# An order of its own for a conv and attention kernel: every engine's line from the kernel's list scheduler

## The chip, the cores and the metric

The kernel runs on one core of one Trainium2 chip. The metric is device time of one launch in microseconds (us). One core has five engines that each work through a line of instructions of their own: TensorE (PE in the profile, its weight loads PEld), VectorE (DVE), ScalarE (ACT), GpSimd (POOL) and SyncE (SP), which here only issues DMAs. Semaphores tie the lines together.

## The reference

The input is 8 images of 384 channels, 32 x 32 (1024 tokens). All is float32. Two layers follow each other:

```
layer 0:  xn = rmsnorm(x);  u, z = xn @ Win            (forward and flipped)
          u = silu(causal_conv4(u));  dt, Bm, Cm = u @ Wx
          delta = softplus(dt @ Wdt + b);  dA = exp(delta * A)
          h[t] = dA * h[t-1] + delta * u * Bm[t]       (16 states per channel)
          y = (sum_n h * Cm + u * D) * silu(z) @ Wout
          x = x + 0.5 * (0.25 * (y_fwd + y_bwd) + sigmoid(dwconv3x3(xn)) * xn)
layer 1:  t = t + attention(layernorm(t))              (6 heads of 64, causal)
          t = t + ffn(layernorm(t))                    (384 -> 1536 -> 384)
```

The FFN's weights are replaced by their signs, and its activations are scaled by a maximum per image group of one; it applies to the first five images only (`FFN_B`), the others get zero. The recurrence over 1024 tokens, two directions, 384 channels and 16 states is the bulk of the elementwise work.

## The kernel before

Channels lie on the 128 partitions in three chunks (c), tokens in two halves of 512 (h). For each image there are three stages.

`before_scan` (L323) does the norm, the in-projection (`in_proj`, L352), the causal conv in both directions d (`conv`, L366; on DVE for image 0, as products with diagonal matrices for the others), Silus, the projection to dt, Bm and Cm (`project`, L500) and `delta` (L530). Its results go to DRAM: u, the Bm and Cm rows (L525), delta and delta*u (L553). `gates` (L460) does the depthwise conv (`local`, L399), z's Silu and the residual.

The scan works in units. One unit covers one image b, one part (direction and half), one chunk c, one group j of four states and one pair q of channel blocks: 128 partitions are 32 channels x 4 states. There are 8 x 4 x 3 x 4 x 2 = 768 units. For each, SP loads delta and delta*u broadcast over states (`s_load`, L587) and the rows (`s_row`, L602); POOL multiplies by Bm (`s_first`, L617), ACT takes two exponentials into PSUM (L630), DVE runs two scans (L638), ACT keeps the carry (L643), POOL multiplies by Cm (L644), PE sums the states of two units by four products that stand on four column strips of the array (`s_sum`, L657), and DVE gates the result (L680, L687). There are six g buffers, so POOL can be ahead of PE by a few units only.

`attention` (L694) and `feed_forward` (L1006) follow an image's scan: out-projection (L723), layernorm, q and k (L756), v (L774), scores of two heads (L816, contraction 64, so each uses half of the array's rows), masked row maximum on DVE (L829), exponential on ACT (L849), transposes (L899), weighted values of two heads (L913), projection (L973); then the two FFN products (L1031, L1075) with their quantization in between and a Gelu (L1054).

What sets the order: every stage hands over a list of steps with rough lengths. The steps of images' other stages are spread between the scan units by due times (end of the kernel function), and each unit's operations get a priority 600 ahead (`ahead_of_all`, L1149). The framework then reorders all instructions by priority in a simulated timeline and assigns buffers in rotation. Here and there `pin` keeps a few instructions in program order, and `at_once` (L269) gives the second product of a pair a head start of 400, so that both come close together. PSUM has eight banks of 128 x 512: two for the scan's exponentials, one for y, and five for the rest by purpose:

```
102:    BANKS = {"y": 1, "da": 2, "s": 2, "pt": 2, "av": 1}
```

The program begins with image 0's `before_scan` alone (only its gates and z are put beside the scan), then runs image 0's scan beside image 1's to 3's `before_scan` and the binarizing of the FFN weights (`binarize`, L207), then the rest; the attention of the last image's second half is last (L1220).

## Time and profile before

| | us |
|---|---|
| median of 3 runs (4350.55 to 4361.42) | 4356.6 |
| the profiled execution | 4362.3 |
| its span, first to last instruction | 4360.0 |
| PE busy | 3692.8 |
| POOL busy | 3596.6 |
| DVE busy | 3378.7 |
| ACT busy | 2805.2 |
| mean granted PE clock (share of full) | 0.876 |

A row of a timeline has the start, the duration, engine, source line, operation, output <- input with shapes, the count merged in that row, and in brackets the idle time before it with what ended it. A row of the waits has who waited for whom, the total, how often and the longest. A row of stretches has from:to, its length, busy time with count for PE, PEld, DVE, ACT and POOL, then the clock, the DMA share and GB/s. A group has its total, and the mean of one in ns. Each float32 product of the PE appears as two matmul records, so an x count of 2 is one product.

### The profile page before, as it was taken

How to read it: one execution, taken by the hardware profiler on the slowest of the kernel's cores; microseconds unless marked ns; L12 is line 12 of the kernel's file. 1: busy time of each engine (PE TensorE's matmuls, PEld its weight loads, DVE VectorE, ACT ScalarE, POOL GpSimd, SP SyncE). 2: the span in 40 equal slices, each digit the busy share in tenths (PEclk: the TensorE clock that was granted, in tenths of full speed). 3: DMA queues.
4: the chain of work that ended last, by engine and by line, in shares of the span. 5: the costliest groups of instructions: out<-in, count | busy, mean ns of one | idle time of the engine just before them, and what ended most of it. 6: DMA issues, size and time to landing. Idle time of an engine off the chain costs nothing.

```text
span 4360.0 us, 43528 instructions
## 1 busy us (share of the span) xinstructions
PE 3692.8 (85%) x12522; PEld 1416.7 (32%) x12522; DVE 3378.7 (77%) x4712; ACT 2805.2 (64%) x5379; POOL 3596.6 (82%) x1560
## 2 busy tenths in 40 slices
PE   3487877898987998779998799898899996999899
PEld 1132322333332333223333233333334332343344
DVE  6899899777988679986789866898877676577723
ACT  4778687676776667765767656677575574575435
POOL 0688989998989988898988998898998989899900
PEclk7686968899987989888999798998889898899899
DMA  6646465422455324463243641346423224224200
GB/s 214 237 162 206 171 231 174 167 95 93 169 193 180 116 78 163 148 230 116 74 163 131 220 150 68 121 148 211 167 91 131 70 92 168 80 83 157 103 15 29
DMA packets 334151, 612.01 MB, mean 140 GB/s; under 512 B 34088, under 2 KB 92888, under 8 KB 333912
## 3 DMA queue, kind: packets, MB, share of 16 engines
q1 hardware_dynamic: 324256, 593.10, 40.0%
q10 hardware_dynamic: 9656, 16.15, 1.1%
q8 instruction: 98, 1.61, 0.2%
q14 instruction: 141, 1.16, 0.1%
HBM read 443.45 MB, written 165.68 MB: 140 GB/s over the span
## 4 chain that ended last, share of the span: by engine, by line
PE 48%; DVE 22%; ACT 6%; issue 5%; POOL 4%; DMA 3%; SPq 0%; DVEq 0%; ACTq 0%; POOLq 0%
DVE g L638 11%; PE s L816 8%; PE yp L1075 6%; PE pt L899 5%; PE qp L756 5%; PE av L913 5%; PE y L657 5%; PE hp L1031 3%; PE op L723 3%; POOL g L617 2%; DVE loc L416 2%; PE in L357 2%; PE ap L973 2%; DVE u L385 2%; POOL g L644 2%
## 5 line engine op out<-in xcount | busy, mean ns | idle before, releaser
L617 POOL TENSOR_TENSOR g<-ud,bc 128x1024 f32<-128x1024 f32 x768 | 1825.1, 2377 | 341.3 <-DMA ud<-sud 131.8
L644 POOL TENSOR_TENSOR g<-g,bc 128x1024 f32<-128x1024 f32 x768 | 1821.9, 2372 | 206.5 <-ACT carry L643 105.1
L630 ACT ACTIVATE da<-dl,amat 128x512 f32<-128x512 f32 x1536 | 1053.2, 690 | 739.7 <-DVE g L638 723.1
L638 DVE TENSOR_TENSOR_SCAN g<-da,carry,g 128x512 f32<-128x512 f32 x768 | 942.9, 1268 | 169.4 <-POOL g L617 120.5
L638 DVE TENSOR_TENSOR_SCAN g<-da,g 128x512 f32<-128x512 f32 x768 | 896.0, 1207 | 147.3 <-POOL g L617 114.5
L816 PE MATMUL s<-k,q 64*128 64x512 f32 (+3 forms) x1152 | 492.9, 608 | 72.0 <-DVE nm L829 70.5
L829 DVE CUSTOM_DVE_ANT_0 pr<-s,cmask 128x512 f32<-128x512 f32 (+3 forms) x576 | 306.1, 551 | 303.1 <-PE s L816 256.4
L657 PE MATMUL y<-g,gather 128*32 128x512 f32 x3072 | 469.3, 687 | 62.0 <-POOL g L644 56.7
L1075 PE MATMUL yp<-h,w 128*128 128x512 f32 x720 | 342.0, 630 | 53.9 <-DVE h L1057 39.9
L902 ACT COPY ptn<-pt 128x512 f32<-128x512 f32 (+3 forms) x576 | 261.6, 477 | 190.2 <-PE pt L899 188.1
L1031 PE MATMUL hp<-t,w 128*128 128x512 f32 x720 | 341.2, 622 | 44.6 <-DMA w<-w1s 22.2
L899 PE MATMUL pt<-ident,pr 128*128 128x128 f32 x1728 | 335.1, 309 | 18.4 <-ACT ptn L902 15.5
L357 PE MATMUL in<-xn,win 128*128 128x512 f32 x576 | 288.8, 647 | 54.1 <-DVE xn L348 18.1
L899 PEld LDWEIGHTS pt<-ident,pr 128*128 128x128 f32 x1728 | 204.5, 150 | 382.6 <-ACT ptn L902 131.6
L537 PE MATMUL dp<-xd,wdt 25*128 25x512 f32 x192 | 162.7, 968 | 154.2 <-ACT du L550 132.9
L416 DVE SCALAR_TENSOR_TENSOR loc<-xn,vec,loc 128x496 f32<-128x496 f32 (+3 forms) x384 | 265.5, 717 | 20.5 <-ACT loc L405 18.6
L849 ACT ACTIVATE pr<-pr,low 128x512 f32<-128x512 f32 (+3 forms) x384 | 241.5, 630 | 53.7 <-DVE low L843 53.1
L913 PE MATMUL av<-ptn,v 128*64 128x512 f32 (+3 forms) x1152 | 265.4, 531 | 1.7 <-ACT ptn L902 1.6
L756 PE MATMUL qp<-t,wqk 128*128 128x512 f32 x576 | 254.8, 597 | 6.8 <-DVE t L318 6.7
L816 PEld LDWEIGHTS s<-k,q 64*128 64x128 f32 x1152 | 165.1, 209 | 263.5 <-DVE nm L829 159.4
L1075 PEld LDWEIGHTS yp<-h,w 128*128 128x128 f32 x720 | 140.7, 201 | 257.7 <-issue 185.9
L1031 PEld LDWEIGHTS hp<-t,w 128*128 128x128 f32 x720 | 136.5, 197 | 246.5 <-issue 150.9
(152 smaller groups left out, 4360.9 us busy)
## 6 DMA issues: line engine op xcount, KB each, us to landing
dl<-sdl SPq DMA_DIRECT2D x384, 256.0 KB, 3.3
ud<-sud SPq DMA_DIRECT2D x384, 256.0 KB, 4.3
bc<-rows SPq DMA_DIRECT2D x256, 256.0 KB, 3.9
su<-u SPq DMA_DIRECT2D x48, 512.0 KB, 3.0
du<-su SPq DMA_DIRECT2D x96, 256.0 KB, 4.4
sdl<-du SPq DMA_DIRECT2D x96, 256.0 KB, 3.5
sud<-du SPq DMA_DIRECT2D x96, 256.0 KB, 3.4
t<-st SPq DMA_DIRECT2D x39, 512.0 KB, 5.2
```

The costliest lines, as they stand in the source:

```text
L357: nc.tensor.matmul(out=mp, lhsT=st["win", c][:, k, i, :], rhs=st["xn"][:, k, half(h)], start=(k == 0), stop=(k == NC - 1),)
L617: pin(nc.gpsimd.tensor_tensor(g, ud, rows_for(u, 0), ALU.mult))
L630: nc.scalar.activation(da, sst["dl", u.b, u.c, u.part, u.q][:, i, :], AF.Exp, scale=amat[:, u.c, k, u.j : u.j + 1],)
L638: nc.vector.tensor_tensor_scan(gi[:, ::step], da[:, ::step], gi[:, ::step], first, ALU.mult, ALU.add)
L644: pin(nc.gpsimd.tensor_tensor(g, g, rows_for(u, 1), ALU.mult))
L657: mm = nc.tensor.matmul(out=y[k * BLK : (k + 1) * BLK, :], lhsT=gather, rhs=pair[k // 2][:, k % 2, :], start=(u.j == u.first_group), stop= ...
L756: nc.tensor.matmul(out=qp, lhsT=st["wqk"][:, c, o : o + P], rhs=st["xn"][:, c, half(h)], start=(c == 0), stop=(c == NC - 1),)
L816: mm = nc.tensor.matmul(out=ss[e][:, : k1 - k0], lhsT=st["q"][rows_of(e), c, chunk(qi)], rhs=st["k"][rows_of(e), c, k0:k1], start=True, st ...
L899: nc.tensor.transpose(pt[:, chunk(i)], pr[:, e, chunk(j % QT)], ident)
L913: mm = nc.tensor.matmul(out=av[rows_of(e), cols], lhsT=st["v"][:, j, hd * HD : (hd + 1) * HD], rhs=st["ptn", j, e][:, cols], start=(j == 0 ...
L1031: nc.tensor.matmul(out=hp, lhsT=st["w1"][:, c, chunk(m % 2)], rhs=st["xn"][:, c, half(h)], start=(c == 0), stop=(c == NC - 1),)
L1075: nc.tensor.matmul(out=yp, lhsT=st["w2", k // 6][:, k % 6, :], rhs=st["h", k // NC][:, k % NC, half(h)], start=(k == 0), stop=(k == NF - 1),)
```

## The change

The kernel no longer calls the engines. Its operations go to a recorder (`Plan`), which notes for each the tiles it reads and writes, its place in the program as a rank (minus the head start that `hurry` gives), and a price in us. `place` then simulates the five engines: at each moment a free engine takes the ready operation of lowest rank whose buffers are to be had; `emit` issues the result in that order, with the framework's own reordering off. Operations recorded under `together` are one unit: the four y products, the two score products, the two weighted-value products, the two projections, each group of Silus or Gelus with the table load behind it. The order of the y products is now 0 to 3. Buffers are given out by the plan too: a free one of the kind, not the next in rotation, within a window of as many tiles as the pool has (PSUM may go beyond the window when one more is free).

The five banks "s", "pt" and "av" become one kind, "any". Operations named `nc.any` go to whichever of ACT and DVE takes them first.

Image 0 gets a `lead`: the norm, in-projection, conv, Silu, projection and delta of half 0, forward, stand alone at the beginning; all else of image 0 goes beside its scan. For this u and the rows are stored by halves (`keep_u`, `keep_rows`), and x is loaded by halves.

```diff
+class Op:
+    def __init__(self, name, what, args, kwargs, rank):
+        self.name, self.parts, self.rank = name, [(what, args, kwargs)], rank
+        self.before, self.behind, self.left = {}, [], 0
+        self.tiles = []
+        self.ready, self.start, self.end = 0.0, None, None
+        self.time = 0.0
+
...
+
...
+    def together(self):
+        self.group = []
+        yield
+        self.group = None
+
...
+    def record(self, name, what, args, kwargs):
...
+        if self.group:
+            op = self.group[0]
+            op.parts.append((what, args, kwargs))
+        else:
+            op = Op(name, what, args, kwargs, len(self.ops) - self.sooner)
+            self.ops.append(op)
+            if self.group is not None:
+                self.group.append(op)
...
+            op.time = max(op.time, cost)
+        else:
+            op.time += cost
+        for v in views:
+            t, box = v.tile, v.box()
...
+                t.order = len(t.kind.queue)
+                t.kind.queue.append(t)
+            for other, b in t.writes + (t.reads if write else []):
+                if other is not op and not (b[1] < box[0] or box[1] < b[0] or b[3] < box[2] or box[3] < b[2]):
+                    op.before[id(other)] = other
...
+    def cost(self, name, what, args, kwargs, written, views):
+
+        if what == "dma_start":
+            n = max(v.free() * v.shape[0] for v in views)
+            return n * 4 / 250e3
+        n = max([v.free() for v in views] or [0])
+        if what == "preload_act_table_set":
+            return 2.6
+        if name == "tensor":
+            return 2 * max(written[0].free(), 64) * 0.00084 / 0.9 + 0.01
+        if name == "gpsimd":
+            return 0.05 + n * 0.00221
+        if name == "scalar":
+            return 0.15 + n * 0.00087 + (0.1 if "accum_out" in kwargs else 0.0)
+        if what == "tensor_tensor_scan":
+            return 0.095 + n / 480
+        if what == "tensor_scalar" and n > HB:
+            return 0.09 + n * 0.00082
+        return (0.17 if "accum_out" in kwargs else 0.085) + n / 960
...
+    def place(self):
+        engines = self.ENGINES
+        waiting = {e: [] for e in engines}
+        ready = {e: [] for e in engines}
+        free_at = {e: 0.0 for e in engines}
+        count = itertools.count()
+        events, dma_free, done = [], 0.0, []
+
...
+        def release(op):
+            op.ready = max(
+                [b.end + (0.0 if b.name == op.name and not b.dma else self.SIGNAL) for b in op.before.values()],
+                default=0.0,
+            )
+            for e in names(op):
+                heapq.heappush(waiting[e], (op.ready, next(count), op))
+                heapq.heappush(events, (op.ready, next(count), e))
+
...
+        def fits(op, now, held):
+            need = {}
+            for t in op.tiles:
+                if t.place is None:
+                    need.setdefault(id(t.kind), []).append(t)
+            for ts in need.values():
+                k = ts[0].kind
+                if k in held:
+                    return False
+                beyond = max(t.order for t in ts) >= k.freed + k.bufs
+                if beyond and k.space != PSUM:
+                    return False
+                if sum(at <= now for at, _ in k.free) < len(ts) + beyond:
+                    if not beyond:
+                        held.add(k)
+                    return False
+            return True
+
...
+            now = events[0][0]
...
+                        if op.start is None:
...
+                            item = heapq.heappop(ready[e])
+                            if item[2].start is not None:
+                                continue
+                            if fits(item[2], now, held):
+                                op = item[2]
+                                break
+                            aside.append(item)
+                        for item in aside:
...
+                        op.name, op.start, moved = e, now, True
...
+                                k = t.kind
+                                k.free.sort()
+                                t.place = k.free.pop(0)[1]
+                        if op.dma:
+                            free_at[e] = now + 0.06
+                            dma_free = max(dma_free, now + 1.5) + op.time - 2.8
+                            op.end = dma_free + 1.3
+                        else:
+                            op.end = free_at[e] = now + op.time
+                        heapq.heappush(events, (free_at[e], next(count), e))
+                        done.append(op)
+                        for t in op.tiles:
+                            users_left[id(t)] -= 1
...
+    def emit(self):
+        def mapped(v):
+            return self.real(v, v.tile.place) if isinstance(v, View) else v
+
+        with self.tc.manual_schedule():
+            for op in self.place():
+                engine = getattr(self.tc.nc, op.name)
+                for what, args, kwargs in op.parts:
+                    if what == "tensor_copy" and op.name == "scalar":
+                        what = "copy"
+                    getattr(engine, what)(
+                        *[mapped(v) for v in args], **{k: mapped(v) for k, v in kwargs.items()}
+                    )
+
...
-    mid = ctx.enter_context(tc.tile_pool(name="mid", bufs=10))
-    ptp = ctx.enter_context(tc.tile_pool(name="ptp", bufs=2))
-    sp = ctx.enter_context(tc.tile_pool(name="scan", bufs=2))
-    dram = ctx.enter_context(tc.tile_pool(name="dram", bufs=5, space=DRAM))
-    ps = ctx.enter_context(tc.tile_pool(name="ps", bufs=1, space=PSUM))
...
+    together, hurry = plan.together, plan.hurry
+    const = Pool(plan, "const", 1, bass.MemoryType.SB)
+    small = Pool(plan, "small", 4, bass.MemoryType.SB)
+    big = Pool(plan, "big", 6, bass.MemoryType.SB)
+    mid = Pool(plan, "mid", 10, bass.MemoryType.SB)
+    ptp = Pool(plan, "ptp", 2, bass.MemoryType.SB)
+    sp = Pool(plan, "scan", 2, bass.MemoryType.SB)
+    dram = Pool(plan, "dram", 5, DRAM)
...
 
-    BANKS = {"y": 1, "da": 2, "s": 2, "pt": 2, "av": 1}
-    turn = [0]
+    BANKS = {"y": 1, "da": 2, "any": 5}
 
     def bank(name, tag=None):
-        if tag is None:
-            turn[0] += 1
-            tag = ("s", "pt")[turn[0] % 2]
+        tag = tag if tag in BANKS else "any"
...
 
...
+        at_half = (emit if lead is None else lead, emit)
+
+        @at_half[0]
         def _():
 
             st["xn"] = btile(f"xn_{b}")
-            load(st["xn"], x[b].rearrange("(c p) l -> p c l", p=P))
+            given = x[b].rearrange("(c p) l -> p c l", p=P)
+            if lead is None:
+                load(st["xn"], given)
+            else:
+                for h in range(NH):
+                    load(st["xn"][:, :, half(h)], given[:, :, half(h)])
...
+        def project_parts(c, h, parts):
+            xp = bank_of(f"xp_{b}_{c}_{h}_{len(parts)}_{parts[0]}")
+            with together():
+                for d in parts:
+                    nc.tensor.matmul(
+                        out=xp[d * DW : (d + 1) * DW, :],
+                        lhsT=wx[:, c, :],
+                        rhs=st["u", d, c][:, half(h)],
+                        start=True,
+                        stop=True,
...
+            else:
+                nc.vector.tensor_tensor(xd, xd, xp[rows, :], ALU.add)
+
+        def keep_u(c, d, h):
+            if (b, "u", d, c) not in spilled:
+                spilled[b, "u", d, c] = dram.tile(
+                    [P, L], F32, name=f"su_{d}_{b}_{c}", tag=f"sp_u_{d}_{c}"
+                )
+            nc.sync.dma_start(out=spilled[b, "u", d, c][:, half(h)], in_=st["u", d, c][:, half(h)])
+
+        def keep_rows(d, h):
+            if (b, "rows", d) not in spilled:
+                spilled[b, "rows", d] = dram.tile(
+                    [2 * NS, L], F32, name=f"rows{d}_{b}", tag=f"rows{d}"
+                )
+            nc.sync.dma_start(
+                out=spilled[b, "rows", d][:, half(h)],
+                in_=st["xd"][d * DW + BC0 : (d + 1) * DW, half(h)],
+            )
...
+            @lead
...
+            for c in range(NC):
+                lead(lambda c=c: in_proj(c, 0, 0), 2.6)
+                lead(lambda c=c: conv(c, 0, 0), 3.0)
+
+            @lead
+            def _():
+                with together():
+                    for c in range(NC):
+                        u = st["u", 0, c][:, half(0)]
+                        nc.scalar.activation(u, u, AF.Silu)
+                    nc.scalar.preload_act_table_set(LOG_EXP)
+                for c in range(NC):
+                    keep_u(c, 0, 0)
+
+            for c in range(NC):
+                lead(lambda c=c: project_parts(c, 0, (0,)))
+            lead(lambda: keep_rows(0, 0))
...
@@ -652,9 +1022,9 @@
             sst["y"] = bank(f"y_{u.name}", "y")
         y = sst["y"]
...
-        for k in (2, 3, 0, 1):
-            with at_once(k != 2):
-                mm = nc.tensor.matmul(
+        with together():
+            for k in range(4):
...
                     out=y[k * BLK : (k + 1) * BLK, :],
                     lhsT=gather,
                     rhs=pair[k // 2][:, k % 2, :],
@@ -662,8 +1032,6 @@
                     stop=(u.j == u.last_group),
                     skip_group_check=True,
                 )
-            if k != 2:
-                pin(mm)
 
     def s_gate(u):
...
-                order = (1, 0)
-                for e in order:
-                    with at_once(e == order[1]):
-                        mm = nc.tensor.matmul(
+                with together():
+                    for e in range(2):
+                        nc.tensor.matmul(
                             out=ss[e][:, : k1 - k0],
                             lhsT=st["q"][rows_of(e), c, chunk(qi)],
                             rhs=st["k"][rows_of(e), c, k0:k1],
                             start=True,
                             stop=True,
                         )
...
                 mask = cmask[:, HB - w :] if k1 == n else cmask[:, :1].to_broadcast([P, w])
...
-                for e in (1, 0):
-                    hd = 2 * c + e
-                    with at_once(e == 0):
-                        mm = nc.tensor.matmul(
+                with together():
+                    for e in range(2):
+                        hd = 2 * c + e
+                        nc.tensor.matmul(
                             out=av[rows_of(e), cols],
                             lhsT=st["v"][:, j, hd * HD : (hd + 1) * HD],
                             rhs=st["ptn", j, e][:, cols],
...
@@ -1180,8 +1544,10 @@
 
     beside = Steps()
     begin = Steps()
-    before_scan(ORDER[0], ("s", "pt"), begin, beside)
+    more = Steps()
+    before_scan(ORDER[0], ("s", "pt"), beside, more, lead=begin)
     run(begin)
+    beside += more
     beside += steps_of(before_scan, ORDER[1], ("s", "pt"), diags=diags)
     beside += steps_of(binarize, w1, w1s, NC, FF, 2, "w1")
...
@@ -1218,6 +1584,7 @@
     for _, _, f in sorted(timed, key=lambda e: e[:2]):
         f()
     run(late)
+    plan.emit()
...
             nc.dram_tensor(f"in_{name}", v.shape, mybir.dt.from_np(v.dtype), kind="ExternalInput").ap()
         )
     args.append(nc.dram_tensor("out_0", (B, C, L), F32, kind="ExternalOutput").ap())
-    with tile.TileContext(nc, schedule_with_timeline_sim=True) as tc:
```

## The prediction

> **What bounds the kernel now.** I read the page's totals first: no engine is full (PE 85%, POOL 82%, DVE 77%), so neither a busy share nor one engine's work gives the time. Next, GpSimd in order of time, because it carries 1536 equal products and every scan unit passes through it twice.
>
> ```profile
> PE 3692.8 (85%) x12522; PEld 1416.7 (32%) x12522; DVE 3378.7 (77%) x4712; ACT 2805.2 (64%) x5379; POOL 3596.6 (82%) x1560
> ```
>
> ```profile
> 8.22 7.00 POOL L1174 TENSOR_SCALAR taps<-ident,vec 128x128 f32<-128x128 f32 x12 [6.32 <-DMA vec<-in_vecs]
> 142.66 4.64 POOL L617 TENSOR_TENSOR g<-ud,bc 128x1024 f32<-128x1024 f32 x2 [127.44 <-DMA ud<-sud]
> ...
> 4148.89 2.36 POOL L644 TENSOR_TENSOR g<-g,bc 128x1024 f32<-128x1024 f32 x1 [1.80 <-DVE g L638]
> ```
>
> These two rows cut the span in three: a head of 142.7 us before the first scan product, a stretch of 4008.6 (142.7 to 4151.3), a tail of 208.7. Back to back, POOL starts one product each 2.310 us (39 starts from 4049.95 to 4140.04). 1536 of them are 3548, so the stretch holds 460 us of lost POOL time. What ends its waits:
>
> ```profile
> POOL g L617 <- DMA ud<-sud: 131.8, 7, 127.4
> POOL g L617 <- PE y L657: 121.4, 75, 5.0
> POOL g L644 <- ACT carry L643: 105.1, 67, 11.1
> POOL g L644 <- DVE g L638: 71.3, 57, 10.0
> ```
>
> The first is the head. The second is a full ring of six g buffers: the y products that free them stand late in PE's line. The next two are scans that come late through ACT and DVE. Last, stretches (PE, PEld, DVE, ACT, POOL busy, clock) and the score products during attention:
>
> ```profile
> 142.00:4151.00 4009.00, 3438.66 (x11631) 1306.72 (x11632) 3230.20 (x4387) 2641.26 (x5035) 3587.98 (x1536) 0.88 0.42 143
> 4151.00:4231.00 80.00, 75.56 (x302) 34.78 (x302) 20.51 (x65) 33.18 (x90) 0.26 (x1) 1.00 0.05 17
> 4231.00:4360.00 129.00, 122.14 (x492) 55.22 (x492) 38.32 (x126) 59.49 (x157) 0.00 (x0) 1.00 0.07 25
> ```
>
> ```profile
> 893.58 1.12 PE L816 MATMUL s<-k,q 64*128 64x512 f32 x2
> 896.50 0.70 PE L816 MATMUL s<-k,q 64*128 64x256 f32 x4
> ...
> 905.73 3.30 PE L816 MATMUL s<-k,q 64*128 64x512 f32 x6 [1.21 <-DVE nm L829]
> ```
>
> The tail is 94% PE. A product is two records; x4 in 0.70 is a pair sharing the array, x6 in 3.30 is three products one after another. Most scores run alone: 146 of the 288 widest stand as x2 at a median 1.12.
>
> **What the skill says.** *TensorE: Matmul & The Clock Gate*, "Part 3: Packing small matmuls — row/col tiling": products on different row or column groups of the array run concurrently, about one product's span for the pack. The 0.70 us pair agrees. *TensorEngine Tiling (Array Packing)*, "Restrictions and Gotchas": different row tiles write different PSUM banks, so a score pair needs two free banks. The trace agrees: PE's weight loads for s waited 159.4 us for DVE's row maximum L829, which frees them. *TensorE*, "Architectural detail: the array is 16× 32×32, not 1× 128×128": ACT and DVE are strictly first in, first out; hence what an order places ahead of a scan is paid by the scan.
>
> **The change, part by part.**
>
> *Head.* Only half 0, forward, of image 0 stands ahead of the first product now; the old order did both halves, both directions and most of the weights' binarizing (some 39 us of DVE). ACT's first square stays at 16.2, behind its own DMA issues. Half a normalisation: xn at 25 (old row). Three in-products of 3 x 0.86 from 24: last at 32. Copy 0.6, scale 0.7, three taps of 0.68, bias 0.7: 36.4. Table 1.28, three Silus of about 0.6, table 1.28: 41. Three projections and two adds: 43. From here SP decides: the rows store lands after 5.0, then eight row loads, which took 11.9 in the old head, are issued ahead of the delta stores (slots rank first): about 61. The delta chain (2 for its product, 8 on ACT and DVE) ends at 53, hidden under SP. Store landing 3.5, ud load 4.3 and its issue: 70, and 2 for filler work in the way: **72**. Bounds 60 (rows land at once) and 95 (a 3.3 us binarizing op ahead of each of several steps). Gain 71. The rest of image 0 moves beside the scans. Part 2 is due 24 units x 4.62 = 111 later; DVE needs 35 for it and has 111 - 24 x 2.4 = 53. That room is its cover; without it POOL would stop for the 35. Added: six u stores, two row stores, one x load, all image 0, under POOL's work on SP: 0.
>
> *Joint products.* If each score pair runs at the cost of one product (1.12, 0.91, 0.70, 0.49 by width; 144 and three times 48 pairs), PE is busy 262 instead of 492.9: -231. The xp pairs take 85.4 for 48; at y's 1.06 that is 51: -34. The y sets (469.3 for 384, 1.22 each against 1.06) and av (265 for 288 pairs) are joint already: 0. The bound from below is 0, should the banks of a pair come free at different times. The unit adds a wait: both products wait for the later bank, and behind them on PE stand y and, for it, POOL. Cover is a third to fifth bank; without it 288 x 0.68 (the other half's L829) = 196 goes back onto PE. None of this is on the path by itself, except in the tail.
>
> *Five banks.* The sum of banks stays 2+2+1. Gains lie where one stage had only its own: dp waited 132.9 for du L550. In softmax, pt and av still hold three. I take nothing beyond what stands below.
>
> *Silu units.* The old line let scan exponentials in between Silus:
>
> ```profile
> L450 ACT ACT_TABLE_LOAD x46 | 59.0, 1283 | 0.8
> L630 ACT ACT_TABLE_LOAD x42 | 53.9, 1283 | 0.8
> ```
>
> All table loads are 129; as units they are about 67: -62 x 1.283 = -80 of ACT. Against it, ACT is shut for 7 us per gate (24 times) and 14 per Gelu; scans wait, POOL runs ahead on up to six g buffers, 4 x 2.31 = 9. Net 0, bounds -40 and +30.
>
> *The list itself* replaces the timeline order; ranks and the 600 of head start for scans stay. It prices POOL rightly (2.313), DVE at 0.62 per 512 where rows show 0.68 to 0.74, scans at 1.16 (rows 1.2), ACT exponentials at 0.595 (row 0.69). Where it fills DVE to its own 100%, one unit's 4.62 holds two scans and 2.30 of other work; on the chip that is 2.40 + 2.30 x 1.12 = 4.98, 0.36 late. Other DVE work is 1540, by its price 1375, of 768 x 2.30 = 1766 room: 78% of units filled, 598 x 0.36 = 215 of POOL stalls. To it I add 46 that no wait explains today (POOL ops stretched, such as 3.87 for 2.35 beside the 128x3072 DVE op), and 70 for y, half of today's 121.4 and rounding up, since 265 us leave PE's line. Stretch: 3548 + 331 = 3879, **-130**. Bounds: 200 of stalls (slack absorbs most of the lag) and 520.
>
> *Tail.* Attention of the last image's half 0, due before the last scans, ran from 4151 to 4231 because PE was on the previous FFN until 4110. With 265 less on PE I credit half of these 80, and 4 of the score pairs in half 1: **-44**; bounds -84 and +16.
>
> *Sum* against the profiled execution (span 4360.0, 2.3 more around it): 72 + 3879 + 165 = 4116 span, 4118 with the rest. The median of the runs is 5.7 below the profiled time: **4112**.
>
> **Rivals.** (1) *The lag is on three engines.* ACT lags as DVE does, transposes are priced at 0.249 against 335.1/864 = 0.39, and the stretch's 130 are lost; head and tail remain: 4242. For it: carry L643 already costs 105.1. Against it: PE and ACT get shorter by 265 and 80. (2) *Loads come late, and it is slower.* The list ends a 256 KB load 1.05 us after issue and, at that size, holds back nothing behind it; the trace has 3.3 to 4.4, and 4.9 to 5.7 for FFN weights priced at 1.57. Place: products right behind a load. 60 weight loads x 3.7 = 222, 16 gate-to-attention hand-overs x (5.8 - 2.1) = 59, 96 changes of scan tiles x 2.75 = 264: 545 if nothing hides. From 245/545 = 45% unhidden it is slower than before; at 60%, 327: 4439. For it: weight tiles share ten buffers, so no early issue is sure. Against: scan loads go out four units (18 us) ahead, and today hp waited for w1s only 22.2. (3) *POOL hardly waits:* 150 of stalls, tail 125: 72 + 3698 + 125 = 3895, by median 3892. DVE would be 85% busy; nothing in the profile shows an order that good. (4) *No change:* head gain eaten by later stages, 4357.
>
> **How the numbers follow.** Forecast 0.58 (own range 4000 to 4220), lag 0.16, late loads 0.17, hardly waiting 0.07, no change 0.02. 0.3% (13 us) is about what this kernel's measurement can tell from none. Faster 0.58 + 0.16 + 0.07 = 0.81, same 0.02, slower 0.17. The range leaves out most of (3) and the upper two thirds of (2): 3960 to 4400.
>
> **What would show it.** First L617 near 72; scores busy near 262 and mostly x4; table loads near 67; "POOL <- PE y" near 60; PE after POOL's end about 165. The prediction is wrong if PE waits on weight loads rise above 100, if carry and g together exceed 200, or if the first product starts after 95.

## The result, and the profile after

The changed kernel took 4336.8 us (median of 7 runs, 4333.4 to 4346.2) beside 4357.4 for the kernel before in the same session (median of 7): a ratio of 0.9944, 95% interval 0.9921 to 0.9968. That is 20 us faster where 245 were forecast. The span of the profiled execution went from 4360.0 to 4338.6.

In the changed kernel every operation is issued from one line of the source, so rows are told apart by the names of their tiles: `scan_g` is g, `ps_any` is a bank of the shared kind, `ps_y` the sum over states. First the busy totals, then GpSimd in order of time, then what ended its waits:

```profile
PE 3639.0 (84%) x12522; PEld 1382.7 (32%) x12522; DVE 3493.6 (81%) x4789; ACT 2689.9 (62%) x5243; POOL 3603.2 (83%) x1560
```

```profile
6.00 6.98 POOL L359 TENSOR_SCALAR big_big<-const_ident,const_vec 128x128 f32<-128x128 f32 x12 [4.11 <-DMA const_vec<-in_vecs]
76.32 2.34 POOL L359 TENSOR_TENSOR scan_g<-scan_ud,scan_bc 128x1024 f32<-128x1024 f32 x1 [63.35 <-DMA scan_ud<-dram_sp_ud]
...
4058.09 7.21 POOL L359 TENSOR_TENSOR scan_g<-scan_g,scan_bc 128x1024 f32<-128x1024 f32 x3
```

```profile
POOL scan_g L359 <- ACT scan_carry L359: 146.3, 48, 12.9
POOL scan_g L359 <- DVE scan_g L359: 112.5, 38, 14.0
POOL scan_g L359 <- DMA scan_ud<-dram_sp_ud: 101.3, 5, 63.3
POOL scan_g L359 <- PE ps_y L359: 65.1, 19, 9.3
```

The first scan product starts 66 us earlier, as forecast. The last one ends 86 us earlier. Both are gains, and they are not what reaches the end: behind the last scan product 273.3 us are left, where there were 208.8.

The forecast added up three stretches: the head, the stretch of scan products, the tail. The result becomes readable once the middle one is cut at 1200 us, when the attention of image 0 has just ended in the changed kernel (its last projection begins at 1179; before at 1052) and the preparation of the first images lies behind. These are the two kernels in such stretches (from:to, length, busy time with count of PE, PEld, DVE, ACT and POOL, clock, DMA share, GB/s), before and after:

```profile
142.66:1200.00 1057.34, 853.77 (x2600) 304.09 (x2601) 929.39 (x1185) 775.72 (x1366) 954.42 (x407) 0.85 0.48 164
1200.00:4151.25 2951.25, 2585.15 (x9033) 1002.76 (x9032) 2301.06 (x3203) 1864.92 (x3668) 2633.82 (x1130) 0.89 0.40 135
4151.25:4360.00 208.75, 197.45 (x794) 89.87 (x792) 58.58 (x190) 92.67 (x247) 0.01 (x1) 1.00 0.06 22
```

```profile
76.32:1200.00 1123.68, 792.85 (x2375) 272.44 (x2376) 941.70 (x1163) 704.43 (x1266) 897.19 (x380) 0.78 0.47 162
1200.00:4065.30 2865.30, 2562.48 (x9151) 983.54 (x9149) 2429.69 (x3340) 1862.40 (x3698) 2697.67 (x1157) 0.94 0.42 142
4065.30:4338.60 273.30, 256.97 (x959) 118.20 (x957) 94.26 (x240) 98.44 (x243) 0.00 (x0) 0.99 0.10 36
```

A scan product takes 2.31 us back to back, so the time that POOL lost in a stretch is its length less 2.31 for each product in it. Before: 1057.3 - 407 x 2.31 = 117 up to 1200 us and 2951.3 - 1130 x 2.31 = 341 after. Changed: 1123.7 - 380 x 2.31 = 246 and 2865.3 - 1157 x 2.31 = 193. So:

| term | before | changed | difference | forecast |
|---|---|---|---|---|
| head, to the first scan product | 142.7 | 76.3 | -66 | -71 |
| POOL time lost from there to 1200 us | 117 | 246 | +129 | } -130 |
| POOL time lost after 1200 us | 341 | 193 | -148 | } |
| tail, after the last scan product | 208.8 | 273.3 | +65 | -44 |
| sum (the span, 4360.0 to 4338.6) | | | -20 (measured -21) | -245 |

The steady part alone did better than the -130 of the forecast. Nearly all that it and the head gained went back in two places for which the sum had nothing, or the other sign: the first stage and the tail.

The other claims about single rows. The score products, by width, and the table loads:

```profile
L359 PE MATMUL ps_any<-big_big,big_big 64*128 64x512 f32 x576 | 186.6, 645 | 6.1 <-ACT ptp_ptn L359 2.3 <-ACT mid_mid L359 1.8 <-DVE small_nm L359 0.7
...
L359 PE MATMUL ps_any<-big_big,big_big 64*128 64x384 f32 x192 | 47.1, 514 | 4.1 <-DVE small_nm L359 2.8 <-ACT big_big L359 1.3
...
L359 PE MATMUL ps_any<-big_big,big_big 64*128 64x256 f32 x192 | 33.9, 403 | 0.2
L359 PE MATMUL ps_any<-big_big,big_big 64*128 64x128 f32 x192 | 31.6, 329 | 11.6 <-DVE small_nm L359 5.7 <-DVE big_big L359 4.6
```

```profile
1054.66 0.92 PE L359 MATMUL ps_any<-big_big,big_big 64*128 64x384 f32 x4
1060.77 1.13 PE L359 MATMUL ps_any<-big_big,big_big 64*128 64x512 f32 x4
```

```profile
L359 ACT ACT_TABLE_LOAD x67 | 86.0, 1283 | 5.3 <-DVE small_qs L359 3.4 <-PEq L1629 0.7
```

Such pairs stand as x4 in the time of one product (1.13 us at 512 columns). The four rows add up to 299 us, against 319.2 + 94.8 + 68.5 + 46.5 = 529 in the same rows before: -230. The forecast's -231 was reckoned from 492.9, where the time in which two widths overlap counts once; counted that way the changed kernel has 285, which is -208. Table loads are 67, as forecast. Yet PE is busy only 54 us less, because the y products went from 469 to 648 us; what that is worth is the first experiment.

PE's granted clock is higher too (0.94 after 1200 us, 0.89 before the change). That is not what sets the time: the list alone (e9 below) had the clock of the changed kernel, 0.90 to 0.91, and took 65 us more.

### The profile page after: what moved, and what is told of

Read it like the earlier page. It is cut to its first block, busy times and chain, and to the rows that moved or that the text cites. A ratio compares the mean times of both kernels' runs of the same rounds, so it can differ in the third digit from the quotient of the medians.

```text
span 4338.6 us, 43725 instructions
## 1 busy us (share of the span) xinstructions
PE 3639.0 (84%) x12522; PEld 1382.7 (32%) x12522; DVE 3493.6 (81%) x4789; ACT 2689.9 (62%) x5243; POOL 3603.2 (83%) x1560
## 4 chain that ended last, share of the span: by engine, by line
POOL 19%; PE 11%; DVE 11%; issue 6%; ACT 2%; DMA 2%; SPq 0%; POOLq 0%; DVEq 0%; ACTq 0%
POOL scan_g L359 19%; PE ps_any L359 10%; DVE scan_g L359 5%; DVE ps_any L359 2%; DVE mid_mid L359 1%; PE ps_y L359 1%; ACT mid_mid L359 1%; DVE big_big L359 1%; DVE small_mxh L359 1%; ACT big_big L359 1%; DMA scan_ud<-dram_sp_ud 0%; DMA dram_sp_dl<-mid_mid 0%; ACT ps_da L359 0%; DMA dram_sp_t<-big_big 0%; ACT L359 0%
## 5 line engine op out<-in xcount | busy, mean ns | idle before, releaser
L359 POOL TENSOR_TENSOR scan_g<-scan_g,scan_bc 128x1024 f32<-128x1024 f32 x768 | 1856.2, 2422 | 285.9 <-ACT scan_carry L359 146.3
L359 POOL TENSOR_TENSOR scan_g<-scan_ud,scan_bc 128x1024 f32<-128x1024 f32 x768 | 1868.1, 2439 | 171.6 <-DMA scan_ud<-dram_sp_ud 99.7
L359 ACT ACTIVATE ps_da<-scan_dl,const_amat 128x512 f32<-128x512 f32 x1536 | 1052.4, 689 | 753.6 <-DVE scan_g L359 720.3
L359 DVE TENSOR_TENSOR_SCAN scan_g<-ps_da,scan_carry,scan_g 128x512 f32<-128x512 f32 x768 | 942.1, 1267 | 167.6 <-POOL scan_g L359 130.9
L359 PE MATMUL ps_any<-big_big,mid_mid 128*128 128x512 f32 x2016 | 966.1, 629 | 131.8 <-ACT mid_mid L359 59.5
L359 DVE TENSOR_TENSOR_SCAN scan_g<-ps_da,scan_g 128x512 f32<-128x512 f32 x768 | 898.6, 1208 | 182.4 <-POOL scan_g L359 149.2
L359 PE MATMUL ps_y<-scan_g,const_gather 128*32 128x512 f32 x3072 | 648.0, 668 | 154.5 <-POOL scan_g L359 140.4
L359 PEld LDWEIGHTS ps_any<-big_big,mid_mid 128*128 128x128 f32 x2016 | 386.0, 199 | 712.5 <-issue 473.6
L359 PE MATMUL ps_any<-big_big,big_big 128*128 128x512 f32 (+4 forms) x1728 | 544.0, 555 | 24.6 <-DVE small_nm L359 9.2
L359 PE MATMUL ps_any<-const_ident,mid_mid 128*128 128x128 f32 x1728 | 306.4, 302 | 66.4 <-DVE small_nm L359 32.4
```

The lines of the kernel that those rows point to most:

```text
L359: getattr(engine, what)(*[mapped(v) for v in args], **{k: mapped(v) for k, v in kwargs.items()})
```

## The experiments

The same four terms, read in the same way from each kernel's profile, are the thread through all of them. Ratios are to the kernel before, measured on the same chip in the same session; its median lay between 4357 and 4372 over the sessions, so kernels of different sessions are compared to about 10 us. Head and tail are in us, and "lost" is POOL's lost time as above.

| kernel | median us | ratio, 95% interval | head | lost to 1200 | lost after | tail |
|---|---|---|---|---|---|---|
| before | 4357.4 | 1 | 143 | 117 | 341 | 209 |
| changed | 4336.8 | 0.9944 (0.9921-0.9968) | 76 | 246 | 193 | 273 |
| e1 y order | 4339.4 | 0.9947 (0.9931-0.9964) | 74 | 246 | 195 | 274 |
| e2 DMA price | 4348.4 | 0.9960 (0.9949-0.9971) | 89 | 219 | 214 | 275 |
| e3 no lead | 4298.1 | 0.9857 (0.9832-0.9882) | 108 | 172 | 190 | 274 |
| e4 banks split | 4447.1 | 1.0196 (1.0171-1.0221) | 80 | 226 | 276 | 310 |
| e5 banks split, no lead | 4413.5 | 1.0109 (1.0079-1.0140) | 122 | 147 | 279 | 312 |
| e6 scores apart | 4368.9 | 1.0009 (0.9996-1.0022) | 76 | 256 | 203 | 291 |
| e9 list alone | 4401.9 | 1.0090 (1.0073-1.0108) | 120 | 158 | 260 | 312 |
| e7 no lead, signs in head | 4282.5 | 0.9803 (0.9772-0.9835) | 129 | 145 | 190 | 274 |
| e10 e7, 300 places ahead | 4284.6 | 0.9824 (0.9804-0.9843) | 129 | 154 | 228 | 221 |
| e18 e7, 585 places ahead | 4301.6 | 0.9859 (0.9816-0.9901) | 128 | 150 | 196 | 275 |
| e8 e7, delta in SBUF | 4520.3 | 1.0350 (1.0321-1.0378) | 134 | 218 | 340 | 273 |
| e11 e7, first tap on DVE | 4349.5 | 0.9972 (0.9961-0.9983) | 124 | 157 | 244 | 274 |
| e16 e7, no sum of u | 4250.8 | 0.9734 (0.9692-0.9777) | 137 | 125 | 166 | 273 |
| e17 e7, sum through PSUM | 4303.6 | 0.9855 (0.9820-0.9890) | 143 | 152 | 183 | 273 |

### Is PE's line the bound? (e1)

```diff
-            for k in range(4):
+            for k in (2, 3, 0, 1):
                 nc.tensor.matmul(
                     out=y[k * BLK : (k + 1) * BLK, :],
```

> One edit to the changed kernel: the four y products of a unit are issued 2, 3, 0, 1 again, so that the first of them needs the g that comes last. Theory A (PE's line is the bound of the other stages, and since the first two y products start on the earlier g, PE then stands before the third until POOL delivers the later one): y busy falls from 648 to about 470 us, PE's wait for POOL from 140 to under 60, and the time by 80 to 150, to 4190 to 4260. Rival B (the list's prices for DRAM round trips set the pace): y busy falls all the same, the time by less than 20.

The y row of the changed kernel and of this one:

```profile
L359 PE MATMUL ps_y<-scan_g,const_gather 128*32 128x512 f32 x3072 | 648.0, 668 | 154.5 <-POOL scan_g L359 140.4 <-DVE scan_yt L359 7.1 <-DVE scan_z L359 5.7
```

```profile
L359 PE MATMUL ps_y<-scan_g,const_gather 128*32 128x512 f32 x3072 | 463.5, 680 | 308.4 <-POOL scan_g L359 297.0 <-DVE scan_yt L359 7.2 <-DVE scan_z L359 3.1
```

Of four products side by side, two read the earlier g and two the later. In the order of the change the first two start and PE then stands, as "busy", until POOL brings the other g. Turned round, 184 us of busy time become 157 us of waiting for POOL, and the time does not move (4339.4 against 4336.8). PE's busy time is nothing to go by here. Theory A falls. The same edit on e7 did nothing either:

> The signs binarized beside image 0's preparation (4282 us), and the y products' four parts in the order 2, 3, 0, 1 of the kernel before, which took 147 us from PE's busy time and nothing from the time of the changed kernel. Theory (the time that PE stands with the first two of four started is a wait for POOL that only changes its name): 4282, within 8. Rival (with less beside image 0's scan PE's line comes onto the path): 4240 to 4270.

It took 4288.1 (ratio 0.983, 0.9812 to 0.9849), with losses of 136 and 192 and a tail of 272.

### Are loads issued too late because DMAs are priced too low? (e2)

```diff
-            return n * 4 / 250e3
+            return 2.8 + n * 4 / 250e3
```

> One edit to the changed kernel: a DMA of 256 KB is priced at 3.85 us from issue to landing (2.8 more than now), as the profile shows 3.3 to 4.4, and transfers then follow each other at 250 GB/s. Rival B: the scan's first 580 us, in which POOL fell 17 products behind the kernel before, get these back, the 32.6 us hole at 198 to 234 shrinks to under 15, and the time falls by 40 to 110, to 4230 to 4300. Theory A: POOL is ahead at 580, but the end moves by less than 20, since the tail's PE work stays; y busy stays near 648.

It was 11 us slower, not faster: the first scan product moves from 76 to 89. The loads' price is not where the time went. The forecast's slower rival falls with it: in the changed kernel all of PE's waits for a DMA add up to 7.4 us, and those of its weight loads to 10.4.

### The lead (e3)

```diff
-    before_scan(ORDER[0], ("s", "pt"), beside, more, lead=begin)
+    before_scan(ORDER[0], ("s", "pt"), begin, more)
```

> One part of the change undone: image 0 is prepared whole before its scan, as in the kernel before; all else as in the changed kernel. Theory A: the first scan product comes near 140 instead of 76, but POOL's end is not what ends the kernel, so the time is within 25 of the changed kernel, 4315 to 4360. If the head were on the path, it would be 66 longer, near 4400.

Without the lead the kernel is 39 us faster, more than the theory's 25 and against the other reading's sign. The lead brings the first product 32 us forward and costs 74 of POOL's time before 1200 (172 to 246). The longest single piece of that in the changed kernel, on GpSimd and then on PE:

```profile
194.81 6.97 POOL L359 TENSOR_TENSOR scan_g<-scan_g,scan_bc 128x1024 f32<-128x1024 f32 x3
234.38 2.34 POOL L359 TENSOR_TENSOR scan_g<-scan_ud,scan_bc 128x1024 f32<-128x1024 f32 x1 [32.60 <-DMA scan_ud<-dram_sp_ud]
```

```profile
212.50 2.07 PE L359 MATMUL ps_any<-mid_mid,const_wdt 25*128 25x512 f32 x2 [0.79 <-DVE mid_mid L359]
222.04 2.07 PE L359 MATMUL ps_any<-mid_mid,const_wdt 25*128 25x512 f32 x2 [7.48 <-ACT mid_mid L359]
245.62 1.92 PE L359 MATMUL ps_y<-scan_g,const_gather 128*32 128x512 f32 x4 [21.50 <-POOL scan_g L359]
```

At 202 the prepared half is used up and POOL stands for 32.6 us. The next half's delta products (`const_wdt`) are only then on PE, at 212 and 222; each is followed by ScalarE, VectorE, a store to DRAM and a load back before POOL can go on. The engines had room: from 200 to 234 VectorE was busy 8 of 34 us, and from 150 to 300 94 of 150, against 139 in the kernel before. In this hole it is the length of a chain of dependent steps, not an engine's load, that the lead left uncovered.

The hole is only the smaller half. It eats what the lead gained in the head: by 300 us POOL has started 76 scan products with the lead and 74 without. The loss that is left comes after it. From 300 to 850 us, with the lead and without:

```profile
300.00:850.00 550.00, 407.69 (x1019) 143.03 (x1016) 503.10 (x570) 354.20 (x574) 386.67 (x160) 0.80 0.56 195
```

```profile
300.00:850.00 550.00, 406.08 (x1032) 135.94 (x1030) 504.05 (x565) 344.49 (x561) 423.28 (x178) 0.79 0.56 196
```

POOL makes 18 products fewer, 42 us of its time, while VectorE is just as busy (503 and 504 of 550). VectorE runs 160 scans there instead of 175, and 171 terms of the depthwise convolution instead of 152: other work stands where scans stood. With split banks (e4 and e5, next) the lead costs 34 us although there is no hole: POOL waits for no load between its first product and 300 us and has started 83 products by then, against 75. It makes 162 from 300 to 850, against 182. So the open chain alone does not explain the cost. That the work moved beside the scan takes VectorE's time in a stretch that has little to spare fits both pairs; no run shows that it is the cause.

### The shared banks (e4, e5)

```diff
-    BANKS = {"y": 1, "da": 2, "any": 5}
+    BANKS = {"y": 1, "da": 2, "s": 2, "pt": 2, "av": 1}
+    turn = [0]
...
-        tag = tag if tag in BANKS else "any"
+        if tag is None:
+            turn[0] += 1
+            tag = ("s", "pt")[turn[0] % 2]
...
```

> One part of the change undone: PSUM banks by purpose again (two s, two pt, one av), with the list and the joint products kept. Theory A: little on PE's line changes, since joint score products need two banks and have two; within 30 of the changed kernel, 4320 to 4365. A rival, that sharing the banks is what costs (a long holder takes the bank that the next product of the other stage needs): 30 or more faster than the changed kernel, under 4305.

> Both parts undone together: image 0 is prepared whole before its scan, and the seven banks beside ps_y are split again 2, 2, 2, 1; the list and the joint products stay. Theory (the lead costs 41 us, the shared banks are worth 110, and the two are independent): 4447 - 41 = 4406, within 12. Rival 1 (the lead hurts only because the shared banks fill with image 0's rest): no gain from leaving it out, 4447. Rival 2 (the list and the units alone are worth something against the order before): below 4340. At 4406 the list with its units would by itself be some 40 us slower than the kernel before, and the gain of the change comes from the banks alone.

Split banks cost 110 us with the lead and 115 without it, where the first expectation had 30 at most, or a gain; the second came within 8 us (4406 forecast). So the two parts hardly depend on each other, and sharing is the largest gain of the change. It lies after 1200 us (-83 and -89) and in the tail (-37 and -38); before 1200 us sharing costs 20 and 25. GpSimd's waits from 1200 us to its end, with split and with shared banks, both without the lead:

```profile
POOL scan_g L359 <- PE ps_y L359: 93.0, 21, 14.4
POOL scan_g L359 <- ACT scan_carry L359: 74.5, 30, 10.7
POOL scan_g L359 <- DVE scan_g L359: 67.9, 33, 12.1
POOL scan_g L359 <- issue: 21.1, 5, 7.9
```

```profile
POOL scan_g L359 <- ACT scan_carry L359: 73.0, 30, 6.9
POOL scan_g L359 <- DVE scan_g L359: 51.0, 24, 7.8
POOL scan_g L359 <- PE ps_y L359: 25.4, 9, 9.0
POOL scan_g L359 <- issue: 12.7, 6, 3.6
```

It is above all the y products that come late with split banks: 93 against 25 us. They need none of these banks themselves. The longest of these waits, on PE and then on GpSimd, in the split kernel without the lead (e5):

```profile
1253.26 4.14 PE L359 MATMUL ps_pt<-big_big,mid_mid 128*128 128x512 f32 x6 [2.55 <-ACT mid_mid L359]
1257.20 7.47 PE L359 MATMUL ps_s<-big_big,mid_mid 128*128 128x512 f32 x16
1264.60 1.07 PE L359 MATMUL ps_y<-scan_g,const_gather 128*32 128x512 f32 x8
```

```profile
1246.73 4.67 POOL L359 TENSOR_TENSOR scan_g<-scan_ud,scan_bc 128x1024 f32<-128x1024 f32 x2
1265.81 4.69 POOL L359 TENSOR_TENSOR scan_g<-scan_ud,scan_bc 128x1024 f32<-128x1024 f32 x2 [14.40 <-PE ps_y L359]
```

The last g was ready at 1247; the sum that frees it is at 1264.6, behind a product into a "pt" bank that stood for ScalarE and a row of others, in an order fixed beforehand. POOL pays for the bank through PE's line.

### Joint score products, and the list alone (e6, e9)

```diff
-                with together():
-                    for e in range(2):
+                for e in range(2):
...
```

> The two score products of a pair are recorded one by one, no longer a unit; all else as in the changed kernel. They lose their joint runs: PE busy rises by up to 230 us (the 529 against 299 us of the score rows). Theory (PE's throughput binds only outside the first stage and in the tail, products that take longer also hold their shared bank longer): slower by 30 to 90, 4370 to 4430. Rival 1 (PE's line is nowhere the bound, as taking 147 us of y products away suggested): within 10 of 4339. Rival 2 (PE binds everywhere): slower by more than 150, above 4490.

> The list alone: image 0 prepared whole, the seven banks split 2, 2, 2, 1, and the score products recorded one by one. Theory (the parts add up: 4414 measured with joint products, and 30 us for taking the joint score products apart, as measured on the changed kernel): 4444, within 15; the list's order alone is then some 80 us slower than the kernel before, and banks and units more than win it back. Rival 1 (with split banks the score products are limited by their banks and not by their length): 4414. Rival 2 (PE's line binds once the banks are split): above 4500.

Recorded one by one in the changed kernel, the score products cost 32 us, 17 of them in the tail. But the edit takes little of the joining away. The widest row of e6:

```profile
L359 PE MATMUL ps_any<-big_big,big_big 64*128 64x512 f32 x576 | 208.6, 665 | 7.2 <-DVE small_nm L359 3.6 <-ACT ptp_ptn L359 1.9 <-ACT mid_mid L359 1.3
```

The four rows are 344 us, against 299 as units and 529 before, because the list mostly puts the two products side by side by itself. So e6 gives back 45 of the 230 us, and what the whole is worth in time no run shows. With split banks recording them apart cost nothing (4401.9 against 4413.5 with joint ones), though the rows rise from 347 to 445 us. So the effect is not additive, and an estimate for e9 by adding was 42 off.

e9 completes a chain of four kernels from the one before to the changed one, and the four terms of each step add up to the result (units are the operations recorded together, Silus and joint projections among them; the sums are differences of spans; the terms are rounded):

| step | head | lost to 1200 | lost after | tail | sum |
|---|---|---|---|---|---|
| the list and all units but the scores | -22 | +41 | -81 | +103 | +41 |
| joint score products | +1 | -11 | +19 | 0 | +9 |
| five shared banks | -14 | +25 | -89 | -38 | -115 |
| lead for image 0 | -32 | +74 | +3 | 0 | +44 |
| all | -66 | +129 | -148 | +65 | -21 |

The list by itself makes the kernel slower; the banks that it can hand out at will more than pay for it; the lead takes a good part away again.

### The tail and the scan's head start (e10)

```diff
-            with hurry(offset=600):
+            with hurry(offset=300):
```

> The signs binarized beside image 0's preparation (4282 us), and the scan's units ranked 300 places ahead of what was recorded around them instead of 600. Theory (work is only shifted: what the scan is served first, the matrix products pay after its end): the last POOL product 15 to 40 us later than its 4014, the tail behind it shorter by as much, the time within 10 of 4282. Rival 1 (the scan's start of 600 is too much and the tail's backlog is pure loss): 4240 to 4265. Rival 2 (the scan sets the pace and needs the start): above 4300.

This kernel and those from here on have no lead, and the FFN weights are binarized beside image 0's preparation (e7, below). With half the head start POOL ends 47 us later and the tail is 53 us shorter; the time is the same. PE after the last scan product, in the changed kernel; then this kernel's tail as one stretch:

```profile
4073.32 10.46 PE L359 MATMUL ps_any<-big_big,mid_mid 128*128 128x512 f32 x24
4084.56 10.57 PE L359 MATMUL ps_any<-big_big,mid_mid 128*128 128x512 f32 x24 [0.78 <-ACT big_big L359]
4095.91 10.57 PE L359 MATMUL ps_any<-big_big,mid_mid 128*128 128x512 f32 x24 [0.78 <-ACT big_big L359]
```

```profile
4060.94:4281.50 220.56, 208.31 (x851) 98.09 (x849) 85.27 (x235) 83.56 (x234) 0.00 (x0) 0.99 0.12 44
```

Six such groups of an FFN's products, 67 us to 4140, are left over when the scan of the changed kernel is done, and the last attention follows them. In the kernel before these products had ended at 4110, 41 us ahead of the scan's end. PE is 91 to 95% busy in the tail in all these kernels, so its length goes with the number of products left: 794 records before, 959 in the changed kernel, 851 here. What the scan is served first, PE pays after it: a tail longer by some 50 us and an earlier end of the scan are two sides of one choice.

### What is left of the first stage (e7, e13, e15, e11, e16, e17, and a control, e18)

```diff
-    before_scan(ORDER[0], ("s", "pt"), beside, more, lead=begin)
-    run(begin)
+    before_scan(ORDER[0], ("s", "pt"), begin, more)
+    signs = steps_of(binarize, w1, w1s, NC, FF, 2, "w1")
+    signs += steps_of(binarize, w2, w2s, NF, C, 8, "w2")
+    run(begin, signs)
     beside += more
     beside += steps_of(before_scan, ORDER[1], ("s", "pt"), diags=diags)
-    beside += steps_of(binarize, w1, w1s, NC, FF, 2, "w1")
-    beside += steps_of(binarize, w2, w2s, NF, C, 8, "w2")
```

> Image 0 is prepared whole before its scan, and the FFN weights are binarized beside that preparation instead of beside image 0's scan. Theory (too much is served beside image 0's scan; the binarizing, its weight loads and its VectorE operations are part of it): the first scan product moves from 108 to about 125, image 0's scan takes 40 us less than the 594 of the run without the lead, attention 0 ends near 1095 instead of 1138, and the time is 4270 to 4285. Rival 1 (the first stage is bound by the preparation of images 1 to 3 and the PSUM banks, the binarizing lies beside it): the head's delay of some 15 us comes on top, 4310 to 4320. Rival 2 (the first stage is bound by one engine's total, so the place of the work within it is nothing): 4298.

Binarizing in the head costs 21 us there and saves 27 behind it: 4282.5 (ratio 0.9803). The time is as the theory had it, the reason only in part: the last projection of image 0's attention begins at 1130, where attention 0 was to end near 1095 (without the edit it begins at 1138). Among the kernels that compute everything it is the fastest, with e10, e12 and e14 within 6 us of it.

Next, whether VectorE sets the pace. It had gained 115 us of busy time, 46 of them copies of q, k and v that the list puts on it when ScalarE is not free first:

```diff
-                        nc.any.tensor_copy(st["qk"[s]][:, m, half(h)], qp)
+                        nc.scalar.copy(st["qk"[s]][:, m, half(h)], qp)
...
-                nc.any.tensor_copy(st["v"][:, j, :], vp[:, :C])
+                nc.scalar.copy(st["v"][:, j, :], vp[:, :C])
```

> The changed kernel with the copies of q, k and v out of PSUM all on ScalarE, instead of on whichever of ScalarE and VectorE the list finds free (81 of 160 on VectorE, 49.7 us; in the kernel before 6 of 160, 3.8 us). Theory (VectorE's work lies on the scan's path: POOL waits for the scans and their carries, which stand behind it; 37 us added cost 67, 278 added cost 238): VectorE's busy time falls by about 48, POOL's waits for the scan and the carry (258.8) by 40 or more, the time to 4260 to 4300. Rival 1 (the copies fill VectorE's gaps; what cost 67 was another thing): within 10 of 4337. Rival 2 (ScalarE, which forms the decays, becomes the late one): 4350 or more.

> The same copies on ScalarE, with image 0 prepared whole before its scan and the FFN weights binarized beside that preparation (4282 us). Theory (as before, and independent of the first stage): 4225 to 4255. Rival (no room is left once the first stage is mended): within 10 of 4282.

> The list alone (image 0 prepared whole, seven banks split 2, 2, 2, 1, score products one by one: 4402 us) with the copies of q, k and v on ScalarE. Theory (VectorE's added work is what makes the list's own order slower than the kernel before's): 4345 to 4370, the time before. Rival (it is the order itself, with scans served before products): 4395 to 4410.

Nothing in any of the three: 4336.2, 4285.7 and 4403.5. GpSimd's waits in the first of them:

```profile
POOL scan_g L359 <- ACT scan_carry L359: 144.3, 47, 13.0
POOL scan_g L359 <- DVE scan_g L359: 111.6, 38, 14.0
```

VectorE has 42 us less to do (3451.9), and POOL waits as before for the scans and their carries. These copies, beside attention, lay in VectorE's gaps.

The other way round, work put on VectorE in the images' preparation:

```diff
-            nc.scalar.activation(
-                acc, st["xn"][:, c, half(h)], AF.Copy, scale=vec[:, c, V_DW + 4 : V_DW + 5]
+            nc.vector.tensor_scalar(
+                acc, st["xn"][:, c, half(h)], vec[:, c, V_DW + 4 : V_DW + 5], None, ALU.mult
             )
```

> The signs binarized beside image 0's preparation (4282 us), and the first of the depthwise convolution's terms is formed by VectorE instead of ScalarE, so that the PSUM bank is taken when VectorE comes to it and not tens of us before. Theory (banks taken early keep products waiting): a depthwise bank is held some 35 us instead of some 59 on average, attention 0 ends by 1110 instead of 1130, and the time is 4255 to 4272. Rival 1 (nobody waits for these banks): 4282, within 8. Rival 2 (VectorE is the busiest engine of the first stage, 142 of 150 us, and the moved work is on its path): 4290 to 4310.

And work taken from it there: the sum of u left out, then made in halves with one operand in PSUM:

```diff
-                usum = mtile(f"us_{b}_{c}")
-                nc.vector.tensor_tensor(usum, st["u", 0, c], st["u", 1, c], ALU.add)
+                usum = st["u", 0, c]
```

> The signs binarized beside image 0's preparation (4282 us), and the sum of the two directions' u left out: its 24 VectorE additions of 128x1024 from SBUF and SBUF (68 us in that run, 2.83 each) are not made, u of the first direction is spilled in its place, so part of the scan's direct term is missing from the output. Theory (VectorE is on the path where images are prepared, there it is busy 138 us of 150, and not where attention runs, where taking 46 us away gave nothing): 20 to 70 below, 4210 to 4260. Rival (VectorE is on the path nowhere; the 67 us lost by moving the depthwise term came from a change of order): 4272 to 4290.

```diff
-                nc.vector.tensor_tensor(usum, st["u", 0, c], st["u", 1, c], ALU.add)
+                for h in range(NH):
+                    t = bank(f"usp_{b}_{c}_{h}")
+                    nc.scalar.copy(t, st["u", 1, c][:, half(h)])
+                    nc.vector.tensor_tensor(
+                        usum[:, half(h)], st["u", 0, c][:, half(h)], t, ALU.add
+                    )
```

> The signs binarized beside image 0's preparation (4282 us), and the same sum made in two halves of 128x512, one of the operands first copied by ScalarE into a PSUM bank, so that VectorE reads SBUF once. Theory (VectorE's additions of two SBUF operands wait for POOL's products; from PSUM and SBUF 128x512 takes 0.68): the sum takes 48 x 0.68 = 33 us instead of 68, ScalarE has 28 us more, and as preparation is on VectorE's path the time is 15 to 40 below, 4240 to 4267. Rival (the added ScalarE copies and banks cost what VectorE gains): 4275 to 4300.

They gave +67, -32 and +21 us against e7 (of the 67, 54 lie after 1200 us). The first two fit a VectorE that sets the pace while images are prepared; the third does not, though its 48 additions did take 0.68 us each. So the control, the same work in another order (600 places to 585):

> A control: the signs binarized beside image 0's preparation (4282 us), and the scan's units ranked 585 instead of 600 places ahead. The work is the same, only the order that the list finds is another. Theory (the list's order itself carries no more than some 10 us of chance): within 10 of 4282, so that the +67 of the moved depthwise term, the -32 of the sum left out and the +21 of the sum through PSUM come from these edits. Rival (any edit has the whole program ordered anew, and that alone moves it by tens of us): 15 or more away from 4282, and differences of this size between two orders have no cause of their own.

It took 19 us more than e7. An edit of any kind has the whole program ordered anew, and in this one control the new order alone was worth 19 us; how much it can be worth at most one control does not say. (Six other edits that hardly change the work, e1, e10 and e12 to e15, moved the time by 1 to 6 us.) The banks (110 and 115) and the lead (39 and 34) were each measured twice, under different orders, and stand; e11 (67) stands well above the control; e16 (32) and e6 (32) stand only just; e17 and e7 against e3 (16) say nothing of their cause. That VectorE sets the pace in the preparation is supported by e11 and e16, and not shown. Why the list by itself loses some 40 us before 1200 stays open: not by the copies (e15), and half the head start hardly changes that loss (145 and 154, e10).

### Holding a PSUM bank for less time (e8)

```diff
-            nc.scalar.copy(dp, w)
-            nc.vector.scalar_tensor_tensor(dp, dp, 1.0, e, ALU.subtract, ALU.subtract)
-            nc.vector.tensor_tensor(dp, dl, dp, ALU.subtract)
-            nc.vector.tensor_tensor(u, u, dp, ALU.mult)
-            nc.scalar.copy(dl, dp)
+            nc.vector.scalar_tensor_tensor(w, w, 1.0, e, ALU.subtract, ALU.subtract)
+            nc.vector.tensor_tensor(dl, dl, w, ALU.subtract)
+            nc.vector.tensor_tensor(u, u, dl, ALU.mult)
```

> As the run before, and the step sizes' last operations work in SBUF: the softplus's remainder is formed in the tile w and not copied back into the PSUM tile dp, so its bank is free after its last read by ScalarE, and two ScalarE copies a set are gone (96 in all). Theory (PSUM banks held by their readers are what the products of the first stage and of the steady stage wait for): 30 to 50 below the run before, some 4240. Rival (the banks are held for other reasons, and VectorE or POOL sets the pace): within 10 of the run before.

It was 238 us slower, where 30 to 50 less or no change was expected. The same three operations in e7 (32 others are in its first row) and here, as groups (total, mean in ns):

```profile
L359 DVE TENSOR_TENSOR mid_mid<-mid_mid,ps_any 128x512 f32<-128x512 f32 x128 | 86.7, 683 | 5.0 <-PE ps_any L359 1.9
...
L359 DVE TENSOR_TENSOR ps_any<-mid_mid,ps_any 128x512 f32<-128x512 f32 x96 | 66.6, 694 | 2.9
L359 DVE SCALAR_TENSOR_TENSOR ps_any<-ps_any,mid_mid 128x512 f32<-128x512 f32 x96 | 65.6, 684 | 19.5 <-ACT ps_any L359 19.2
```

```profile
L359 DVE SCALAR_TENSOR_TENSOR mid_mid<-mid_mid 128x512 f32<-128x512 f32 x96 | 187.5, 1953 | 0.0
...
L359 DVE TENSOR_TENSOR mid_mid<-mid_mid,mid_mid 128x512 f32<-128x512 f32 x96 | 182.3, 1899 | 2.5
L359 DVE TENSOR_TENSOR mid_mid<-mid_mid 128x512 f32<-128x512 f32 x96 | 143.9, 1499 | 2.8
```

From PSUM and SBUF each takes 0.68 to 0.69 us; with both operands in SBUF 1.50 to 1.95. Two operands in SBUF are not slow by themselves. The same three in e8's own head, before POOL's first scan product (0 to 134 us):

```profile
L359 DVE TENSOR_TENSOR mid_mid<-mid_mid 128x512 f32<-128x512 f32 x2 | 1.4, 693 | 0.1
L359 DVE TENSOR_TENSOR mid_mid<-mid_mid,mid_mid 128x512 f32<-128x512 f32 x2 | 1.4, 692 | 0.1
L359 DVE SCALAR_TENSOR_TENSOR mid_mid<-mid_mid 128x512 f32<-128x512 f32 x2 | 1.4, 682 | 0.0
```

They are slow once POOL multiplies. That is 96 x (1.95 + 1.90 + 1.50 - 0.68 - 0.69 - 0.68) = 317 us more of VectorE in these rows, on the way from the projection to the scan's loads (278 in VectorE's whole busy time, 3487.7 to 3765.5). The two ScalarE copies that looked like waste keep VectorE out of POOL's way. About banks the run says nothing.

## Why the prediction was wrong

By the steps of its sum:

- **Head, -71: right in size, by luck.** -66; 76.3 against 72. Two errors cancel. The last projection's sum was done at 58.7, where 43 was forecast (x was normalised at 34 and not at 25, and the taps and Silus lasted until 53 and not 41). From there to the first product it took 17.6 us, where 29 were forecast: the eight row loads were issued in 5.1 us and not 11.9, and the delta chain ended with them, at 66, and was not hidden under them.
- **"The rest of image 0 moves beside the scans ... That room is its cover": this step failed.** It set VectorE's 35 us of work against 111 - 24 x 2.4 us, as if nothing but scans stood there besides, and put the rest at 0. It was not 0 but +74 (e3; +79 with split banks), more than twice what the lead gains in the head against the same kernel without it (-32). In the changed kernel some 32 of it is a chain through PE, ScalarE, VectorE, a store and a load that ended after the scan had used up the prepared half. The other 42 come from 300 to 850 us, where VectorE was 91% busy with or without the lead (501 of 550 us in the kernel before); their cause is not shown.
- **Five banks, "I take nothing": failed.** Sharing is worth 110 to 115 us, the largest term (e4, e5). Its price on POOL comes through PE's line, by the y products behind a product that has no bank, and the step looked only at whose own banks were short.
- **The list, 331 of POOL stalls in place of 460: mis-sized.** The list alone has 158 + 260 = 418. The term for y (70) came out at 65, but by the banks: with split banks it is 93 after 1200 us alone. The 215 for VectorE's lag should be held against the waits for carry and scan, 259 in the changed kernel and 176 before; that they come from prices set too low was not tested.
- **Joint products: near on PE, little of it seen in time.** Scores -208 for -231, counted as the forecast did; the projections -9 for -34 (85.4 to 76.0); "y ... joint already: 0" became +179, which e1 shows to cost nothing. Recording the scores one by one cost 32 us or nothing, but took back only part of the joining.
- **Silu units: right on the count.** 67 table loads. What they do to the time was not taken apart from the list.
- **Tail, "With 265 less on PE I credit half of these 80": failed, in sign.** +65. PE's total does not say what is left when the scan ends; the order does (e10).
- **Rivals.** Late loads (4439) fall by e2. "The lag is on three engines" (4242) had the gain of the stretch lost, and it was nearly lost (+129 - 148 = -19 for -130); its reason, prices set too low, was not tested, and its tail was wrong too. "Head gain eaten by later stages", given 0.02, came nearest in mechanism, for the lead's part. The forecast's own sign of failure, carry and g together above 200, came true: 258.8.

Behind two of these steps stands one choice: the stretch of 4009 us was treated as one. It is two stages that went opposite ways, +129 and -148, and a uniform stall rate cannot see that.

## What to carry to other kernels

Cut the span where the mix of work changes, and for each stage set its length against the work of the engine that paces it; a reordering that wins in the steady part can lose the same in the ramp. An earlier start of the pacing engine is not yet a gain: count the next piece of its input as a chain of steps with its store and load, and ask where the work that was moved away will stand and whether the engines are full there. Here both questions were missed, and the kernel without the early start was 39 us faster. When a list scheduler serves one engine first, look for the bill behind that engine's last instruction; and before a difference of a per cent or less is read as a cause, order the same work anew and see what that alone does.

## What the hardware showed

- VectorE operations with two operands in SBUF, beside GpSimd's products: 1.50 to 1.95 us on average for 128x512, against 0.68 to 0.69 with one operand in PSUM, and the same 0.68 to 0.69 with two in SBUF before GpSimd's first product (e8). The Trainium skill, "SBUF — State Buffer", section "Who interferes with whom", says that "A DVE instruction with two SBUF inputs contends with a GpSimd instruction that reads SBUF"; the trace agrees. POOL's own products were hardly longer for it (2.45 and 2.41 us, against 2.40 and 2.38 in e7, 57 us over all 1536), so here VectorE was the one that paid most.
- A one-input operation is concerned too: `tensor_scalar` on 128x614 from SBUF to SBUF took 0.54 us in e7's head (38 to 49 us), where POOL has no products yet, and 2.18 in the changed kernel (390 to 440 us), beside them. The same section counts `tensor_scalar` among the operations that can enter the 2-port modes and so contend; that it was in such a mode no run here shows.
- A set of products that share the array counts as busy while it stands half started: the y sets read 1.69 us each with the earlier operand's products first, and 1.21 with the later's first (648.0 and 463.5 over 384 sets), at equal time of the kernel.
